# Layer 1's expert outputs: one written row per token and choice, weights loaded by row pairs, early sums fetched by pairs of tiles

## The chip, the cores and the metric

The kernel runs on one core of one Trainium2 chip. The metric is device time in microseconds. A core has five engines that matter here, each with its own instruction queue worked off in order: TensorE (PE, with its weight loads shown apart as PEld), VectorE (DVE), ScalarE (ACT), GpSimd (POOL) and SyncE (SP). SyncE computes nothing: it issues most of the DMAs. GpSimd issues the indirect DMAs, which gather or scatter rows by an index per partition.

## The reference, cut to what matters

Two layers, each of graph attention over a dense mask and then a mixture of experts, on 2708 nodes of 256 features, in fp32. Layer 0's mixture has 8 experts of hidden width 1024, layer 1's has 16 of width 512. A token goes to its two best experts. The part that the change concerns is this:

```python
# layer 1's mixture; x is the layer-normed node, K = 2
topk_vals, topk_idx = jax.lax.top_k(x @ gate_w + gate_b, K)
topk_w = jax.nn.softmax(topk_vals, axis=-1)          # the two weights of a token add up to 1
h = jax.nn.relu(jnp.einsum('bsh,ehf->bsef', x, w1) + b1)
expert_out = jnp.einsum('bsef,efh->bseh', h, w2) + b2
sel = jnp.take_along_axis(expert_out, topk_idx[:, :, :, None], axis=2)
y = x + jnp.sum(topk_w[..., None] * sel, axis=2)
out = (y - mean(y)) / jnp.sqrt(var(y) + EPS) * gamma + beta   # over the features
# and around it: nodes = nodes + out
```

## The kernel before, in words

The 2708 nodes are 22 tiles (T) of up to 128 partitions (P): 20 full ones and two of 74 rows (TAIL). W is 22 x 128 = 2816. Only the two chosen experts of a token are computed. The class `Router` ranks the choices, gives each (token, choice) a place in a list sorted by expert, and scatters a row there, into `rows_d` in DRAM (`scatter`, L681): 256 features and behind them the token's number (column D, from `tail`, L536), the expert and a weight. The list is cut into blocks of 128 rows of one expert each. Layer 0 works through 47 blocks for certain and layer 1 through 45 (`sure`); more would follow only if the data asked for them.

The class `Experts` does a block. `fetch` (L768) brings its 128 rows, `load_w1` (L755) and `load_w2` (L759) the expert's weights into one of three rooms (left out if the same expert is there already). `turn` transposes the rows on TensorE (L468) and ScalarE copies them. `hide` (L887) multiplies by w1, one chunk of 128 hidden columns at a time, its w1 chunk as the stationary operand; `bend` (L891) is the activation on ScalarE. `sum_hidden` (L902 for the bias, L905) multiplies by w2. `weigh` makes from the row's last columns `side` (L879: +0.5 or -0.5, by which of the token's choices this block's expert is) and on ScalarE the weight `w` (L881). `scaled` (L909, L911) makes `yo`, the weighted output, out of the PSUM. `add` (L916) is an indirect DMA on GpSimd which adds the 128 rows into `sums`, at the tokens' numbers. Even and odd blocks have a tensor each, so two chains exist, and within a chain an add waits for the one before it, since both can hold the same rows.

Layer 1's two sums are made by `sums_d` (L514 ff.): the second is filled with a row of nothing for all nodes and the first only for its filler rows (L518, two DMAs, the bigger 2,944 KB). The first gets its start from `store` (L932 to L935), which writes each tile's layer-normed rows, so that the sum of both tensors is x + moe. `points1` calls it (L1873), tile after tile, between attention and routing.

After the stream the rows come back: y_all has a place for each of the two tensors, y_all[:, 0] and y_all[:, 1]. GpSimd adds them (L1963 early, L1998 late), DVE takes mean and variance (L434, L435), a reciprocal root by a chain of small operations, and two operations per tile (L1973 and L1975 early, L2011 and L2013 late) that also add the node. Three parts follow each other: early group 1 (tiles 0 to 5), whose rows are complete after block 35; early group 2 (tiles 6 to 11), complete after block 38; and the late tiles 12 to 21, complete only at the end. Both early groups lie in `early_last` (from L1950), beside the last blocks, and the late ones in `last1` (from L1990). `early_out` (L1984) writes an early group's result.

The order of work on TensorE, ScalarE, DVE and SyncE in layer 1 is fixed when the program is built. `Clock` is a planner: each piece of work is a Python generator that yields an engine with an assumed duration, or a mark to wait for, and the planner places the instructions in the order of its own modelled times. So a figure such as

```python
                yield "DVE", 0.7
                yo = self.scaled(b, ps, weights.pop(b))
```

costs nothing itself but sets where in DVE's queue `scaled` stands. GpSimd's order is left to the scheduler. `experts1.rest()` follows the stream: on all five engines it loads the number of blocks in use (L948) and branches over the rest (L951). What is written behind it, the late loads among them, stands behind that branch in each queue. On SyncE the order at the end is: output writes of group 1, the branch, the ten late loads, the output writes of group 2.

Of the kernel before, what the change touches and what calls it, by code (L numbers as in the profile page):

```python
# [9 lines left out]
F32 = mybir.dt.float32  # L10
# [12 lines left out]
P = 128  # L23
# [123 lines left out]
def kernel(  # L147
# [374 lines left out]
    class Router:  # L522
# [4 lines left out]
        def __init__(self, layer, E, groups, w_gate, b_gate):  # L527
            self.w_gate, self.b_gate, self.E, self.layer = w_gate, b_gate, E, layer
            self.blocks = NB = blocks_of(E)
            self.rows_d = dram.tile([NB * P, RW], F32, name=f"rows_d{layer}")  # L530
            self.logits = sm.tile([P, T, E], F32, name=f"logits{layer}")
            nc.gpsimd.memset(self.logits, 0.0)
            self.hot = sm.tile([P, T, 2, E], BF16, name=f"hot{layer}")
            self.place = sm.tile([P, T, 2], I32, name=f"place{layer}")
            self.tail = sm.tile([P, T, 3], F32, name=f"tail{layer}")
            nc.gpsimd.iota(self.tail.bitcast(I32)[:, :, 0], pattern=[[P, T]], base=0,  # L536
                           channel_multiplier=1)

            self.room, self.page, self.next = (
                kept(f"{name}{layer}", 0.0, E) for name in ("room", "page", "next"))  # L540

            self.ends = sm.tile([P, len(groups), E], F32, name=f"ends{layer}")
            nc.gpsimd.memset(self.ends, 2.0 ** 22)
            self.groups, self.xt, self.ps, self.rows = groups, {}, {}, {}
            self.moves, self.reads, self.done = [], [], 0
# [174 lines left out]
    class Experts:  # L720
# [5 lines left out]
        def __init__(self, layer, router, w1, b1, w2, func, sums, tags, xg, xt, bias, sure):  # L726
# [6 lines left out]
            self.rooms, self.rows, self.known, self.planned, self.stages = {}, {}, 0, 0, []  # L733
            self.last_add, self.adds, self.early_reads = {}, ([], []), ([], [])
            self.b1_rows = w1x.rearrange("p c f -> p (c f)")[:E, :self.F]
            self.taken, self.sure = taken_of[layer], sure
# [18 lines left out]
        def load_w1(self, b):  # L755
            nc.sync.dma_start(self.rooms[b % 3][0], self.w1[bass.ds(self.e, 1)].rearrange(
                "o (c p) f -> p (o c) f", p=P), **self.when)

        def load_w2(self, b):  # L759
            nc.sync.dma_start(self.rooms[b % 3][1], self.w2[bass.ds(self.e, 1)].rearrange(  # L760
                "o (c p) d -> p (o c) d", p=P), **self.when)

# [21 lines left out]
        def plan(self, upto, bank=None):  # L784
# [72 lines left out]
            for f in range(self.FC):  # L857
                nc.tensor.matmul(ps[:, f], self.b1_rows[:, f * P:(f + 1) * P], hot[:E],
                                 start=True, stop=True)
# [9 lines left out]
        def turn(self, b):  # L869
            xt = self.xt_tile()  # L870
            ps = ps_tile("tr_ps", self.t_tag)[:, :D].rearrange("p (c n) -> p c n", n=P)
            nc.scalar.copy(xt, turn_rows(self.rows[b][:, :D], P, ps))
            return xt

        def weigh(self, b):

            xg = self.rows[b]
            side, w = (self.pool.tile([P, 1], F32, name=nm, bufs=3) for nm in ("side", "w"))
            nc.vector.tensor_scalar(side, xg[:, D + 1:D + 2], mine_of[:, b:b + 1], -0.5,  # L879
                                    op0=OP.is_equal, op1=OP.add)  # L880
            nc.scalar.activation(w, xg[:, D + 2:D + 3], AF.Tanh, scale=side)  # L881
            return w

        def hide(self, b, f, xt, ps):
            w1_b = self.rooms[b % 3][0]
            for c in range(DC):
                nc.tensor.matmul(ps[:, :P], w1_b[:, c, f * P:(f + 1) * P], xt[:, c, :],  # L887
                                 start=(c == 0), stop=(c == DC - 1))
# [19 lines left out]
        def scaled(self, b, ps, w):  # L908
            nc.vector.tensor_scalar(w, w, 0.5, 0.5, op0=OP.mult, op1=OP.add)  # L909
            yo = self.pool.tile([P, D], F32, name="yo", bufs=4)  # L910
            nc.vector.tensor_scalar(yo, ps[:, :D], w, None, op0=OP.mult)  # L911
            return yo

        def add(self, b, yo):
            k = b % 2
            ins = nc.gpsimd.indirect_dma_start(  # L916
# [41 lines left out]
        def stream(self, clock, stages, bank, acc, xrs, los, wides, widened, started):  # L958
# [47 lines left out]
            def turn(b):  # L1006
# [3 lines left out]
                yield "PE", 0.4  # L1010
                turn_rows(self.rows[b][:, :D], P, ps)
                clock.start(turned(b, ps, slot), 0)
# [17 lines left out]
            def weigh(b):  # L1030
                yield "DVE", 0.2
                yield "ACT", 0.3
                weights[b] = self.weigh(b)

            def finish(b, ps, slot):
                yield "DVE", 0.7
                yo = self.scaled(b, ps, weights.pop(b))
# [3 lines left out]
                clock.set(xr_slots.pop(b))  # L1041
                clock.set(self.added_at[b], 4.5)

# [656 lines left out]
    emb_sq, sig_sq, common = kept("emb_sq", 1.0), kept("sig_sq", 32.0), kept("common")  # L1700
    router1 = Router(1, E1, groups1, wg1, bg1)
    router1.fill()
    sums1 = [sums_d(f"sums1_{k}", zero=k == 1) for k in range(2)]
    experts1 = Experts(1, router1, L1_ffn_w1, L1_ffn_b1, L1_ffn_w2, AF.Relu, sums1,
# [100 lines left out]
    def points1(group):  # L1805
# [62 lines left out]
        for q, (t, r) in enumerate(group):  # L1868
# [3 lines left out]
            ln_f1.apply_s(router1.rows[t][:r, :D], x1[:r, t, :], t, r, shift[:, q:q + 1])  # L1872
            experts1.store(t, r, router1.rows[t][:r, :D])  # L1873
            if q % 2:
# [70 lines left out]


    EARLY_LAST = ((tiles[:6], 36), (tiles[6:12], 39))
    assert ENDS1[:2] == (6, 12) and list(early1.values()) == [8, 20] and E1 == 16

    def early_last(group, done):  # L1950

        yield experts1.added_at[done - 1]
        mark, lo, n = Mark(), group[0][0], len(group)
        if lo:
            yield experts1.loaded
            yield experts1.fetched
        for k in range(2):
            experts1.early_read(k, fetch_rows(y_all[:, k, lo:lo + n], sums1[k], group), done)
        clock.moved(mark, 0.8 * n, 2.5)
        yield mark  # L1960
        for t in range(lo, lo + n, 2):
            yield "POOL", 1.3
            nc.gpsimd.tensor_tensor(y_all[:, 0, t:t + 2], y_all[:, 0, t:t + 2],  # L1963
# [6 lines left out]
        for t, r in group:  # L1970
# [5 lines left out]
                                           op1=OP.add)  # L1976
        if not lo:
            yield experts1.loaded
            yield experts1.fetched
            early_out(group)  # L1980

    def early_out(group):
        for (t, _), _ in zip(group[::2], group[1::2]):
            nc.sync.dma_start(of_pair(out, t), y_all[:, 1, t:t + 2])  # L1984

    def load_y(group, k):
        lo = group[0][0]
        fetch_rows(y_all[:, k, lo:lo + len(group)], sums1[k], group)

# [47 lines left out]

    for group in late_last:
        load_y(group, SURE1 % 2)
    for group, mark in zip(late_last, loads):  # L2040
        load_y(group, 1 - SURE1 % 2)
        clock.moved(mark, 0.4 * len(group), 2.0)
    early_out(tiles[6:12])
    for group, mark in zip(late_last, loads):
# [33 lines left out]
```

## Time and profile before

| | |
|---|---|
| timed runs, median (lowest to highest) | 1162.97 us (1161.6 to 1166.65), 3 runs |
| profiled execution, its own time | 1136.56 us |
| its span; mean granted TensorE clock | 1134.8 us; 0.958 |
| PE, PEld busy | 1023.5 us (90%), 909.0 us (80%) |
| DVE, ACT, POOL busy | 541.9 us (48%), 572.7 us (50%), 367.1 us (32%) |
| DMA | 238.96 MB, 165,461 packets, mean 211 GB/s |
| L911, `yo`: 92 on DVE | 483 ns each |
| L916, accumulating add: 45 in layer 1, on POOL | 1569 ns each, landing after 4.6 us (median) |
| L887, weight loads, layer 0 (1504) and layer 1 (480) | 193 and 200 ns each |

The profile is of one execution; all its times are microseconds from the span's start. Its stages are, roughly: 0 to 120 the front, 120 to 330 attention of layer 0, 330 to 630 the experts of layer 0, 630 to 880 attention and routing of layer 1 (with routing going on beside the first blocks), 880 to 1094 the experts of layer 1, and 1094 to 1135 the end. The last matmul of the 45th block ends at 1093.84. A row of groups gives busy time and mean duration, and then the idle time that the engine had just before these instructions, with the instruction that ended most of it. A row of waits gives who waited, for what, the total, how many times, and the longest. Since engines overlap, a row's busy time is not its price: that is what it adds to the chain that ends last.

### The profile page before, as it was taken

How to read it: one execution, taken by the hardware profiler on the slowest of the kernel's cores; microseconds unless marked ns; L12 is line 12 of the kernel's file. 1: busy time of each engine (PE TensorE's matmuls, PEld its weight loads, DVE VectorE, ACT ScalarE, POOL GpSimd, SP SyncE). 2: the span in 40 equal slices, each digit the busy share in tenths (PEclk: the TensorE clock that was granted, in tenths of full speed). 3: DMA queues.
4: the chain of work that ended last, by engine and by line, in shares of the span. 5: the costliest groups of instructions: out<-in, count | busy, mean ns of one | idle time of the engine just before them, and what ended most of it. 6: DMA issues, size and time to landing. Idle time of an engine off the chain costs nothing. (4 is left out here: it accounts for less than half of the span.)

```text
span 1134.8 us, 21254 instructions
## 1 busy us (share of the span) xinstructions
PE 1023.5 (90%) x6665; PEld 909.0 (80%) x6665; DVE 541.9 (48%) x2083; ACT 572.7 (50%) x1599; POOL 367.1 (32%) x417
## 2 busy tenths in 40 slices
PE   5999999998999999999999999998984888999950
PEld 3788888886889999999998853898984787898840
DVE  7778888887420111111111235647777552122368
ACT  4867667664524444444443357536754543444320
POOL 7531112111242222212222350253345166433442
PEclk9999999999989999999999999999897889999985
DMA  9965354431889999999899959400225477787974
GB/s 289 288 242 177 136 175 156 166 95 58 303 251 295 327 326 322 323 306 321 257 311 335 340 160 278 150 1 6 76 84 153 124 215 188 187 213 178 282 194 133
DMA packets 165461, 238.96 MB, mean 211 GB/s; under 512 B 11035, under 2 KB 140374, under 8 KB 162632
## 3 DMA queue, kind: packets, MB, share of 16 engines
q1 hardware_dynamic: 146524, 214.09, 57.9%
q0 software_dynamic: 18816, 23.42, 10.6%
q8 instruction: 56, 0.92, 0.3%
q14 instruction: 65, 0.53, 0.2%
HBM read 205.54 MB, written 54.99 MB: 230 GB/s over the span
## 5 line engine op out<-in xcount | busy, mean ns | idle before, releaser
L911 DVE TENSOR_SCALAR yo<-out_ps,w 128x256 f32<-128x256 f32 x92 | 44.5, 483 | 402.4 <-PE out_ps L905 401.9
L1246 PE MATMUL att_ps<-g_all,z 128*128 128x257 f32 (+3 forms) x968 | 223.6, 383 | 0.0
L905 PE MATMUL out_ps<-room,ht 128*128 128x256 f32 x872 | 201.1, 383 | 0.0
L1246 PEld LDWEIGHTS att_ps<-g_all,z 128*128 128x128 f32 (+3 forms) x968 | 174.9, 186 | 29.6 <-issue 3.1
L887 PEld LDWEIGHTS hid_ps<-xt,room 128*128 128x128 f32 x1504 | 176.4, 193 | 7.3 <-issue 2.5
L887 PE MATMUL hid_ps<-xt,room 128*128 128x128 f32 x1504 | 177.7, 277 | 4.2 <-DMA room<-in_L_ffn_W_dram 3.7
L905 PEld LDWEIGHTS out_ps<-room,ht 128*128 128x128 f32 x872 | 162.7, 192 | 21.3
L1232 ACT ACTIVATE zr<-e_bc,minus_one,g_all 128x256 f32<-128x256 f32 (+3 forms) x242 | 130.4, 591 | 46.4 <-DVE z L1235 45.8
L916 POOL DMA_INDIRECT sums<-yo,xg x43 | 66.8, 1554 | 235.0 <-DVE side L879 173.4
L891 ACT ACTIVATE ht<-hid_ps,w_t 128x128 f32<-128x128 f32 x376 | 128.7, 364 | 28.0 <-PE hid_ps L887 8.8
L681 POOL DMA_INDIRECT rows_d<-xr,place x88 | 92.2, 1048 | 121.0 <-DVE xr L450 76.9
L1649 PE MATMUL att_ps<-half,wide_mask 128*128 128x258 f32 (+1 forms) x968 | 124.5, 290 | 2.5 <-ACT h_all L1586 1.5
L1649 PEld LDWEIGHTS att_ps<-half,wide_mask 128*128 128x128 f32 (+1 forms) x968 | 121.5, 195 | 3.9 <-ACT h_all L1586 2.4
L1235 DVE SCALAR_TENSOR_TENSOR z<-zr,mask_t 128x256 f32<-128x256 f32 (+3 forms) x242 | 96.9, 422 | 29.6 <-ACT zr L1232 18.3
L916 POOL DMA_INDIRECT sums<-yo,xr x45 | 70.6, 1569 | 118.0 <-DMA sums<-yo,xr 30.0
L891 ACT ACTIVATE ht<-hid_ps,w1x 128x128 f32<-128x128 f32 x180 | 62.4, 363 | 88.6 <-PE hid_ps L887 85.0
L881 ACT ACTIVATE w<-xg,side 128x1 f32<-128x1 f32 x43 | 12.7, 294 | 169.2 <-DVE side L879 169.2
L1525 POOL CAST wide_mask<-mask_t 128x1408 fp32r<-128x1408 fp8e4 x31 | 42.5, 1375 | 101.6 <-PE att_ps L1649 67.5
L887 PE MATMUL hid_ps<-lo,wide_mask 128*128 128x128 f32 x480 | 63.4, 287 | 5.6 <-DMA wide_mask<-in_L_ffn_w_dram 4.7
L887 PEld LDWEIGHTS hid_ps<-lo,wide_mask 128*128 128x128 f32 x480 | 60.6, 200 | 9.4 <-issue 6.5
L905 PE MATMUL out_ps<-wide_mask,ht 128*128 128x256 f32 x240 | 59.6, 393 | 0.0
L468 PE MATMUL tr_ps<-ident,xr 128*128 128x128 f32 (+1 forms) x214 | 38.2, 289 | 22.2 <-DMA xr<-rows_d 13.9
(292 smaller groups left out, 1325.0 us busy)
## 6 DMA issues: line engine op xcount, KB each, us to landing
room<-in_L_ffn_W_dram SPq DMA_DIRECT2D x94, 1024.0 KB
wide_mask<-in_L_ffn_w_dram SPq DMA_DIRECT2D x60, 512.0 KB
room<-in_adj_dram SPq DMA_DIRECT2D x20, 1354.0 KB
room<-in_L_ffn_w_dram SPq DMA_DIRECT2D x30, 512.0 KB
rows_d<-nobody SPq DMA_DIRECT2D x1, 7511.0 KB
rows_d<-nobody SPq DMA_DIRECT2D x5, 1295.0 KB
sums<-nobody SPq DMA_DIRECT2D x2, 2944.0 KB
xr<-rows_d SPq DMA_DIRECT2D x45, 129.5 KB
```

The costliest lines, as they stand in the source:

```text
L468: nc.tensor.transpose(ps[:, c, :r], src[:, c * P:(c + 1) * P], ident[:r, :r])
L681: ins = nc.gpsimd.indirect_dma_start(out=self.rows_d[:, :], in_=self.rows[t][:r], in_offset=None, out_offset=bass.IndirectOffsetOnAxis(ap= ...
L887: nc.tensor.matmul(ps[:, :P], w1_b[:, c, f * P:(f + 1) * P], xt[:, c, :], start=(c == 0), stop=(c == DC - 1))
L891: nc.scalar.activation(ht[:, f, :], ps[:, :P], self.func, bias=self.bias[:, f, b:b + 1])
L905: nc.tensor.matmul(ps[:, :D], ht[:, f, :], self.rooms[b % 3][1][:, f, :], start=False, stop=(f == self.FC - 1))
L911: nc.vector.tensor_scalar(yo, ps[:, :D], w, None, op0=OP.mult)
L916: ins = nc.gpsimd.indirect_dma_start(out=self.sums[k][:, :], in_=yo, in_offset=None, out_offset=bass.IndirectOffsetOnAxis(ap=self.rows.pop ...
L1232: nc.scalar.activation(zr[:k, :n], e_bc[:k, lo:lo + n], AF.Relu, bias=minus_one[:k], scale=g_all[:k, j, D + 1:D + 2])
L1235: nc.vector.scalar_tensor_tensor(z[:k, :n], zr[:k, :n], 1.0, mask_t[:k, j // 2, lo:lo + n, j % 2], op0=OP.add, op1=OP.mult)
L1246: nc.tensor.matmul(accs[i][:r, :D + 1], z[:k, q * P:q * P + r], g_all[:k, j, :D + 1], start=(j == 0), stop=(j == LAST))
L1525: nc.gpsimd.tensor_copy(m, src)
L1649: nc.tensor.matmul(accs[i][:, :D + 2], wide_masks[i, j % 2][:k, j // 2, :], half_k[:k, j, :], start=(j == 0 and half_k is halves[0]), stop ...
```

## The change

There are four parts.

1. In layer 1 a single DRAM tensor `sums1` of 2W rows takes the place of the two sums. The row of choice k of the node at partition p of tile t is k W + p T + t, so that one partition's tiles lie side by side. `weigh` computes this index (`spot`, on DVE) from `side` and from the row's `tail` column, which now holds p T + t + W/2. `put` is a plain indirect scatter, without adding and without a wait on earlier blocks; filler rows get an index beyond the bound and aren't written. `scaled` gets one more DVE operation, which adds w times the block's input row, because the two weights of a token add up to 1; so the filling of the sums and `store` go.
2. In both layers a partition's share of w1 becomes two neighbouring rows, and of w2 two neighbouring rows per chunk pair, in one run. Transposes, hide and the bias then read every second column of their stationary operand (`turn_row`, `part`).
3. The early sums are fetched two tiles at a time, each pair after a mark one block later than the pair before, both choices in one DMA (`load_y`). Group 2 no longer waits for the end of the loads and fetches before its own loads; both groups wait for it before `early_out`. The late loads are five DMAs in place of ten (the pair of 74 rows is split in two), and the call that wrote group 2's results after them goes: group 2 writes them inside the stream.
4. The planner's assumed durations follow: `weigh` 0.4, `finish` 1.1 on DVE, landing 3.0, and 1.6 for the move of a pair.

```diff
@@ -533,8 +533,12 @@
             self.hot = sm.tile([P, T, 2, E], BF16, name=f"hot{layer}")
             self.place = sm.tile([P, T, 2], I32, name=f"place{layer}")
             self.tail = sm.tile([P, T, 3], F32, name=f"tail{layer}")
-            nc.gpsimd.iota(self.tail.bitcast(I32)[:, :, 0], pattern=[[P, T]], base=0,
-                           channel_multiplier=1)
+            if layer:
+                nc.gpsimd.iota(self.tail[:, :, 0], pattern=[[1, T]], base=W // 2,
+                               channel_multiplier=T, allow_small_or_imprecise_dtypes=True)
+            else:
+                nc.gpsimd.iota(self.tail.bitcast(I32)[:, :, 0], pattern=[[P, T]], base=0,
+                               channel_multiplier=1)
 
             self.room, self.page, self.next = (
                 kept(f"{name}{layer}", 0.0, E) for name in ("room", "page", "next"))
@@ -732,6 +736,7 @@
             self.FC, self.NB = self.F // P, router.blocks
             self.rooms, self.rows, self.known, self.planned, self.stages = {}, {}, 0, 0, []
             self.last_add, self.adds, self.early_reads = {}, ([], []), ([], [])
+            self.spots = {}
             self.b1_rows = w1x.rearrange("p c f -> p (c f)")[:E, :self.F]
             self.taken, self.sure = taken_of[layer], sure
 
@@ -754,11 +759,12 @@
 
         def load_w1(self, b):
             nc.sync.dma_start(self.rooms[b % 3][0], self.w1[bass.ds(self.e, 1)].rearrange(
-                "o (c p) f -> p (o c) f", p=P), **self.when)
+                "o (p c) f -> p (o c) f", p=P), **self.when)
 
         def load_w2(self, b):
-            nc.sync.dma_start(self.rooms[b % 3][1], self.w2[bass.ds(self.e, 1)].rearrange(
-                "o (c p) d -> p (o c) d", p=P), **self.when)
+            room = self.rooms[b % 3][1].rearrange("p (q s) d -> p q (s d)", s=2)
+            nc.sync.dma_start(room, self.w2[bass.ds(self.e, 1)].rearrange(
+                "o (q p s) d -> p (o q) (s d)", p=P, s=2), **self.when)
 
         def load(self, b):
             self.choose(b)
@@ -855,7 +861,7 @@
             ps = ps[:, :self.FC * n].rearrange("p (f b) -> p f b", b=n)
             yield "PE", 0.2 * self.FC
             for f in range(self.FC):
-                nc.tensor.matmul(ps[:, f], self.b1_rows[:, f * P:(f + 1) * P], hot[:E],
+                nc.tensor.matmul(ps[:, f], self.part(self.b1_rows, f), hot[:E],
                                  start=True, stop=True)
             yield "ACT", 0.4
             if not lo:
@@ -869,22 +875,37 @@
         def turn(self, b):
             xt = self.xt_tile()
             ps = ps_tile("tr_ps", self.t_tag)[:, :D].rearrange("p (c n) -> p c n", n=P)
-            nc.scalar.copy(xt, turn_rows(self.rows[b][:, :D], P, ps))
+            nc.scalar.copy(xt, self.turn_row(b, ps))
             return xt
+
+        def turn_row(self, b, ps):
+            by_turns = self.rows[b][:, :D].rearrange("p (n c) -> p c n", c=DC)
+            for c in range(DC):
+                nc.tensor.transpose(ps[:, c], by_turns[:, c], ident)
+            return ps
+
+        def part(self, w, f):
+
+            return w.rearrange("p (q n s) -> p q s n", n=P, s=2)[:, f // 2, f % 2]
 
         def weigh(self, b):
 
             xg = self.rows[b]
             side, w = (self.pool.tile([P, 1], F32, name=nm, bufs=3) for nm in ("side", "w"))
+            if self.layer:
+                self.spots[b] = self.pool.tile([P, 1], I32, name="spot", bufs=5)
             nc.vector.tensor_scalar(side, xg[:, D + 1:D + 2], mine_of[:, b:b + 1], -0.5,
                                     op0=OP.is_equal, op1=OP.add)
             nc.scalar.activation(w, xg[:, D + 2:D + 3], AF.Tanh, scale=side)
+            if self.layer:
+                nc.vector.scalar_tensor_tensor(self.spots[b], side, -float(W), xg[:, D:D + 1],
+                                               op0=OP.mult, op1=OP.add)
             return w
 
         def hide(self, b, f, xt, ps):
             w1_b = self.rooms[b % 3][0]
             for c in range(DC):
-                nc.tensor.matmul(ps[:, :P], w1_b[:, c, f * P:(f + 1) * P], xt[:, c, :],
+                nc.tensor.matmul(ps[:, :P], self.part(w1_b[:, c], f), xt[:, c, :],
                                  start=(c == 0), stop=(c == DC - 1))
 
         def bend(self, b, f, ht, ps):
@@ -909,9 +930,24 @@
             nc.vector.tensor_scalar(w, w, 0.5, 0.5, op0=OP.mult, op1=OP.add)
             yo = self.pool.tile([P, D], F32, name="yo", bufs=4)
             nc.vector.tensor_scalar(yo, ps[:, :D], w, None, op0=OP.mult)
+            if self.layer:
+                nc.vector.scalar_tensor_tensor(yo, self.rows.pop(b)[:, :D], w, yo, op0=OP.mult,
+                                               op1=OP.add)
             return yo
 
+        def put(self, b, yo):
+
+            ins = nc.gpsimd.indirect_dma_start(
+                out=self.sums[0][:, :], in_=yo, in_offset=None,
+                out_offset=bass.IndirectOffsetOnAxis(ap=self.spots.pop(b), axis=0),
+                bounds_check=2 * W - 1, oob_is_err=False)
+            for other in [put for _, put in self.adds[0]] + self.early_reads[0]:
+                tc.declare_no_dep(ins.ins, other, reason="every choice of a token has its row")
+            self.adds[0].append((b, ins.ins))
+
         def add(self, b, yo):
+            if self.layer:
+                return self.put(b, yo)
             k = b % 2
             ins = nc.gpsimd.indirect_dma_start(
                 out=self.sums[k][:, :], in_=yo, in_offset=None,
@@ -1008,7 +1044,7 @@
                 slot = yield from bank.get()
                 ps = ps_tile("tr_ps", self.t_tag)[:, :D].rearrange("p (c n) -> p c n", n=P)
                 yield "PE", 0.4
-                turn_rows(self.rows[b][:, :D], P, ps)
+                self.turn_row(b, ps)
                 clock.start(turned(b, ps, slot), 0)
 
             def turned(b, ps, slot):
@@ -1028,18 +1064,18 @@
                     clock.set(ht_at[b])
 
             def weigh(b):
-                yield "DVE", 0.2
+                yield "DVE", 0.4
                 yield "ACT", 0.3
                 weights[b] = self.weigh(b)
 
             def finish(b, ps, slot):
-                yield "DVE", 0.7
+                yield "DVE", 1.1
                 yo = self.scaled(b, ps, weights.pop(b))
                 clock.set(slot)
                 yield "POOL", 1.6
                 self.add(b, yo)
                 clock.set(xr_slots.pop(b))
-                clock.set(self.added_at[b], 4.5)
+                clock.set(self.added_at[b], 3.0)
 
             def outputs(b):
                 slot = yield from acc.get()
@@ -1699,8 +1735,10 @@
     emb = h_all[:, :, :D]
     emb_sq, sig_sq, common = kept("emb_sq", 1.0), kept("sig_sq", 32.0), kept("common")
     router1 = Router(1, E1, groups1, wg1, bg1)
+    nc.gpsimd.iota(nobody[:, D:D + 1], pattern=[[0, 1]], base=W + W // 2, channel_multiplier=1,
+                   allow_small_or_imprecise_dtypes=True)
     router1.fill()
-    sums1 = [sums_d(f"sums1_{k}", zero=k == 1) for k in range(2)]
+    sums1 = [dram.tile([2 * W, D], F32, name="sums1")]
     experts1 = Experts(1, router1, L1_ffn_w1, L1_ffn_b1, L1_ffn_w2, AF.Relu, sums1,
                        ("wide", "wide", "acc"), lambda b: xr_tile(),
                        lambda: side.tile([P, D], F32, name="lo", bufs=2).rearrange(
@@ -1870,7 +1908,6 @@
             router1.rows[t] = xr_tile()
             yield "ACT", 0.6
             ln_f1.apply_s(router1.rows[t][:r, :D], x1[:r, t, :], t, r, shift[:, q:q + 1])
-            experts1.store(t, r, router1.rows[t][:r, :D])
             if q % 2:
                 clock.start(logits1(group[q - 1:q + 1], taken_at[lo][q // 2]), urgency(group))
         for mark in taken_at[lo]:
@@ -1944,21 +1981,26 @@
 
 
 
+    def load_y(group):
+
+        lo, hi = group[0][0], group[-1][0] + 1
+        src = sums1[0].rearrange("(k p t) d -> p k t d", k=2, p=P)
+        for a, b in parts_of_rows(group[0][1]):
+            ins = nc.sync.dma_start(y_all[a:b, :, lo:hi], src[a:b, :, lo:hi])
+        return ins
+
     EARLY_LAST = ((tiles[:6], 36), (tiles[6:12], 39))
     assert ENDS1[:2] == (6, 12) and list(early1.values()) == [8, 20] and E1 == 16
 
     def early_last(group, done):
 
-        yield experts1.added_at[done - 1]
-        mark, lo, n = Mark(), group[0][0], len(group)
-        if lo:
-            yield experts1.loaded
-            yield experts1.fetched
-        for k in range(2):
-            experts1.early_read(k, fetch_rows(y_all[:, k, lo:lo + n], sums1[k], group), done)
-        clock.moved(mark, 0.8 * n, 2.5)
-        yield mark
+        lo, n = group[0][0], len(group)
         for t in range(lo, lo + n, 2):
+            mark = Mark()
+            yield experts1.added_at[done - 1 + (t - lo) // 2]
+            experts1.early_read(0, load_y(tiles[t:t + 2]), done)
+            clock.moved(mark, 1.6, 2.5)
+            yield mark
             yield "POOL", 1.3
             nc.gpsimd.tensor_tensor(y_all[:, 0, t:t + 2], y_all[:, 0, t:t + 2],
                                     y_all[:, 1, t:t + 2], OP.add)
@@ -1974,18 +2016,13 @@
                                            op0=OP.subtract, op1=OP.mult)
             nc.vector.scalar_tensor_tensor(y, y, ln_y.rstd[:, t:t + 1], x1[:, t, :], op0=OP.mult,
                                            op1=OP.add)
-        if not lo:
-            yield experts1.loaded
-            yield experts1.fetched
-            early_out(group)
+        yield experts1.loaded
+        yield experts1.fetched
+        early_out(group)
 
     def early_out(group):
         for (t, _), _ in zip(group[::2], group[1::2]):
             nc.sync.dma_start(of_pair(out, t), y_all[:, 1, t:t + 2])
-
-    def load_y(group, k):
-        lo = group[0][0]
-        fetch_rows(y_all[:, k, lo:lo + len(group)], sums1[k], group)
 
     def last1(group, y_at):
 
@@ -2035,12 +2072,9 @@
     late_last = [tiles[12:14], tiles[14:16], tiles[16:20], tiles[20:22]]
     loads = [Mark() for _ in late_last]
 
-    for group in late_last:
-        load_y(group, SURE1 % 2)
     for group, mark in zip(late_last, loads):
-        load_y(group, 1 - SURE1 % 2)
-        clock.moved(mark, 0.4 * len(group), 2.0)
-    early_out(tiles[6:12])
+        load_y(group)
+        clock.moved(mark, 0.8 * len(group), 2.0)
     for group, mark in zip(late_last, loads):
         clock.start(last1(group, mark))
     clock.run()
```

## The prediction

> **What bounds the kernel now.** I read the page's span, then busy times cut by stage, then TensorE's waits in each stage, SyncE's waits, and last the timeline of the final 40 us. Busy times by stage (columns: us, then PE, PEld, DVE, ACT, POOL busy, granted clock, DMA share, GB/s):
>
> ```profile
> 330.00:600.00 270.00, 268.42 (x1830) 251.57 (x1830) 27.71 (x113) 113.16 (x360) 55.19 (x37) 0.99 0.96 304
> 900.00:960.00 60.00, 50.43 (x362) 44.80 (x361) 29.51 (x156) 23.09 (x75) 35.91 (x34) 0.94 0.69 179
> 960.00:1090.00 130.00, 124.52 (x851) 114.23 (x851) 39.53 (x148) 56.90 (x189) 53.73 (x35) 0.99 0.82 221
> 1090.00:1135.00 45.00, 3.84 (x20) 2.97 (x17) 30.96 (x95) 3.96 (x12) 14.58 (x11) 0.58 0.50 137
> ```
>
> Both expert streams (rows 1 and 3) belong to TensorE: 268 of 270 us and 125 of 130. DVE is at 40 of 130 us in the second, so DVE work there lies under matmuls. The last 45 us have almost no matmul: DVE, 31 us, carries them. So only two things move the end: what holds TensorE in layer 1's stream, and the order of DVE, SyncE and GpSimd after about 1083 us. TensorE's waits, 880 to 1095 us (total, times, longest):
>
> ```profile
> PE tr_ps L468 <- DMA xr<-rows_d: 13.9, 2, 12.3
> PE hid_ps L887 <- DMA wide_mask<-in_L_ffn_w_dram: 4.7, 4, 3.2
> PE hid_ps L887 <- DMA room<-in_L_ffn_w_dram: 3.5, 5, 1.4
> PE number_ps L826 <- DVE fresh_bf L822: 3.1, 1, 3.1
> ```
>
> The 12.3 us waits for the first rows after the router's scatters and stays. The rest is some 13 us. In layer 0 TensorE waited for weights only 3.7 us in all. SyncE's queue, 780 to 960 us:
>
> ```profile
> SPq L935 <- ACT xr L459: 34.2, 7, 14.9
> ```
>
> Line 935 is `store`: 24 writes of rows into the sums. The last six issue at 920.92 to 928 us, and the next fetch of rows follows at 929.32, ahead of TensorE's second tr_ps wait (1.59 us, at 931.6). The end, SyncE and then DVE:
>
> ```profile
> 1085.56 4.76 SPq L1984 DMA_DIRECT2D out_dram<-mask_t  x3
> 1102.91 1.41 SPq L1428 DMA_DIRECT2D mask_t<-sums  x3
> ...
> 1109.41 4.79 SPq L1984 DMA_DIRECT2D out_dram<-mask_t  x3
> ```
> ```profile
> 1100.37 0.43 DVE L434 BATCH_NORM_STATS2 bn<-mask_t 128x6 f32<-128x256 f32 x1 [6.00 <-POOL mask_t L1963]
> ...
> 1112.42 1.42 DVE L1975 SCALAR_TENSOR_TENSOR mask_t<-mask_t,rstd_y,h_all 128x256 f32<-128x256 f32 x1
> 1113.98 0.43 DVE L434 BATCH_NORM_STATS2 bn<-mask_t 128x6 f32<-128x256 f32 x1
> ```
>
> The ten late loads (1102.91 to 1108.9) go ahead of the three output writes of early group 2 (1109.41), so the late sums are there when DVE finishes group 2, and DVE goes on at 1113.98 with no idle time. That order is what the change turns round.
>
> [...]
>
> **The change, part by part.** The sum is against the profiled 1136.56 us (span 1134.8); the timed median, 1162.97, stands 2.3% above, and I add the difference to it.
>
> *Weights by row pairs (both layers).* Counts don't change. Packets of w1 and w2 halve in number. [...] TensorE is busy 268.42 of 270, so it can return at most the 3.7 us waited: -1 taken (0 to -3.7). [...] Hide's time is about 47 x 3.73 + 45 x 1.95 = 263 us, so each 1% on it is +2.6 us; a read at half speed would be over 100 us. I take 0.
>
> *Puts instead of accumulating adds (layer 1).* L916 takes 1569 ns on GpSimd and lands in 4.6 us; the plain scatter (L681) takes 1048 ns and lands in 3.5 to 3.9. So 45 x 0.5 = 23 us less on POOL, and no 30.0 us of waits. All hidden: POOL is at 54 of 130 us. In the stream: 0.
>
> *DVE pays for it.* Per block, spot (128x1, as side: 0.20 us) and x*w+yo (128x256, as L1936: 0.48), 45 x 0.68 = 31 us. Between 960 and 1090 this makes 40 into 60 of 130 us: cover remains, and yo frees the PSUM before the new line. Between 895 and 910, where the plan of the layer is made and TensorE already waits 3.1 us for DVE's fresh_bf, two blocks' extra may lie in the way: +1.5 (0 to +3).
>
> *Fills and stores.* Two fills (21.4 us of SyncE's issue at 683, with nothing due until 781) and 24 stores go. Hidden, except the SyncE lag of 920 to 929: -1.6 at 931.6 and, if SyncE then keeps its lead, the 3.25 us wait at 956.3 with the slow first hide after it (3.11 against 1.95): -1.6 to -6; I take -3. An added iota on POOL lies in an idle stretch: 0.
>
> *Early loads by pairs.* Six DMAs of 512 KB, spread through w1/w2 of blocks 40 to 44, instead of four of 768 KB. The 1.4 us TensorE wait at 1075.8 stands beside the old ones: -0.7 (0 to -1.4). TensorE's end (1093.8) thus moves by -1 + 1.5 - 3 - 0.7 = about -3, from -10 to +3.
>
> *DVE's order at the end.* Before, group 1 starts its statistics in the gap of block 40 (1075). In the built program they stand after the new line of block 41, about 1083.8, and side and spot of block 43 wait behind them. From there, at the rows' durations (pair statistics 1.22, newton chain 2.3 to 2.4, 0.92 a tile): group 1's statistics to 1088.8 with their waits, newton to 1091.2, blocks 42 to 44 between tiles 0 and 1 to 1096.4, tiles 2 to 5 to 1100.2, group 2's statistics to about 1104.8 with POOL beside them, newton and 12 operations to 1112.6. Before: 1113.9. The 6.00 us wait on POOL vanishes, and group 1's later start eats it: -1.3.
>
> *SyncE's order at the end: the step that decides.* The output writes of both groups now come before the block count's load, the branch over the rest, and the late loads. Queued behind group 2's last write, which waits for DVE (1112.6), are: its issue 0.4; load and branch 0.9 (1090.4 to 1091.3 before); [...], 5.0 us on SyncE before, 1.1 on DVE, 2.9 on POOL, taken as 2.5 (0.5 to 5); issue to landing 2.3; POOL's add of a pair, 1.26. So DVE starts the late part at 1112.6 + 7.4 = 1120.0 instead of 1113.98: +6.0 (+3.5 to +9.5). Five loads instead of ten save only issue time that was hidden. The late part (17.65 us of DVE, then 3.2 to the end) is the same.
>
> Sum: -3 + 6 = **+3 us**, span about 1138; 1162.97 + 3 = **1166 us**. Nearly everything else that the change removes was hidden.
>
> **Rivals.** (a) *Slower by a strided stationary read.* No trace row excludes it[...]. From 2% on hide it decides alone (+5 us); 5% gives +13, 1180 us. It would show as LDWEIGHTS of L887 longer than 193 ns and a layer-0 block above 7.36 us. (b) *Faster through the removed queueing.* If the stores had held SyncE back for the whole ramp, the waits of 1.6, 4.7, 3.5 and the slow hides go (-10), and [...] (+3.5): -7, 1156 us. For: the 929.32 fetch. Against: 4.7 and 3.5 us come in nine pieces, and TensorE is back at 0.96 by 960. (c) *Slower through DVE in the plan chain[...]:* +3 there instead of +1.5, SyncE's saving not realised (0), tail +9.5: +12, 1175 us. [...] (d) *Packets matter in the timed runs.* They are 26 us over the profiled one, unexplained[...].
>
> **How the numbers follow.** A difference under 0.5% (5.8 us) is about what a measurement here can't tell from none. My forecast +3 has 0.50; within it some 0.30 stay inside 0.5%, 0.18 fall above, since the tail's +6 reaches the end whole where upstream savings fail, 0.02 below. (a) 0.12, slower. (b) 0.13, faster. (c) 0.17, 0.15 of it slower. (d) 0.08, 0.07 of it faster. Together faster 0.22, same 0.33, slower 0.45. The range 1152 to 1183 takes in the tail's and the ramp's ends and a 5% stride; left out are a half-speed read (0.08), more than 11 us gained (0.07), and odd waits. The likeliest case alone spans 1161 to 1173.
>
> **What would show it.** Right: a DVE gap of 5 to 8 us between group 2's last operation and the late statistics, ended by POOL's late add, with SyncE's late loads issued after 1113; L916 near 1.0 us; no POOL wait for sums in the stream; LDWEIGHTS of L887 still near 193 ns; layer-0 period 7.36 us; the late part 17 to 18 us. The prediction is wrong if hide's pitch moves (a), if TensorE ends layer 1 more than 7 us earlier (b), or if the 900 to 960 us stretch loses TensorE time to fresh_bf (c).

## The result and the profile after

The changed kernel takes 1192.03 us (median of 4 runs, 1189.6 to 1196.42) against 1164.4 us before (4 runs, 1161.6 to 1166.65): a ratio of 1.0245, with a 95% interval of 1.0214 to 1.0276. It is slower by about 28 us, where the forecast said 3 us slower and a range up to 1183 us. Timed once more beside the kernel before, it came to 1.0201 (1.0168 to 1.0234), some 23 us. The loss is of 2.0 to 2.5%.

The two first profiles can't be subtracted from each other. Kernels were compared on one chip at a time, and the median of the kernel before was 1135.8, 1157.5, 1164.3 and 1136.2 us in the four later comparisons, the first and last of which were on the same chip. The first profile of before (1136.56 us) is like those of the quicker chip, the first of the changed kernel (1189.6 us) like those of the slower ones. So where spans and ends are compared below, and nothing else is said, the traces are the second profiles of both, taken on one chip: 1138.94 and 1157.68 us.

First the changed kernel's busy times by stage, from its first profile (columns as before: us, PE, PEld, DVE, ACT, POOL busy, clock, DMA share, GB/s):

```profile
330.00:600.00 270.00, 267.26 (x1780) 250.86 (x1779) 27.33 (x113) 111.89 (x348) 53.78 (x36) 0.99 0.91 293
960.00:1090.00 130.00, 120.90 (x824) 111.37 (x823) 51.88 (x205) 54.91 (x178) 37.72 (x41) 0.99 0.56 179
1090.00:1135.00 45.00, 39.80 (x264) 36.48 (x262) 24.22 (x79) 17.35 (x57) 14.84 (x15) 0.99 0.76 256
1135.00:1188.00 53.00, 0.00 (x0) 0.00 (x0) 37.40 (x105) 3.28 (x9) 10.91 (x9) 0.50 0.29 104
```

Layer 0's row tells nothing of the cost: TensorE is as busy as before, because it is busy for longer per block. The DMA share is 0.91 in place of 0.96 (0.93 in the second profile), with fewer bytes moved per us (293 in place of 304 GB/s), and it returned nothing. The two middle rows lie in layer 1's expert stream, where DVE, at 52 of 130 us, stays under the matmuls. The last row is the end without matmuls, some 53 us long, of which DVE works 37. The timeline of TensorE in layer 0 shows the first cause, in the first profile of before and then of after; the second profiles have the same durations:

```profile
427.86 3.73 PE L887 MATMUL hid_ps<-xt,room 128*128 128x128 f32 x32
431.43 0.38 PE L468 MATMUL tr_ps<-ident,xg 128*128 128x128 f32 x2
431.65 0.27 PE L902 MATMUL out_ps<-b,hot_of 96*128 96x256 bf16 x1
431.77 3.62 PE L905 MATMUL out_ps<-room,ht 128*128 128x256 f32 x16
```
```profile
430.41 3.92 PE L908 MATMUL hid_ps<-xt,room 128*128 128x128 f32 x32
434.17 0.39 PE L884 MATMUL tr_ps<-ident,xg 128*128 128x128 f32 x2
434.40 0.27 PE L923 MATMUL out_ps<-b,hot_of 96*128 96x256 bf16 x1
434.51 3.62 PE L926 MATMUL out_ps<-room,ht 128*128 128x256 f32 x16
```

Hide's 32 matmuls, which now read w1 at a step of two, take 3.92 us and not 3.73. The matmuls with w2, whose stationary operand is not strided, stay at 3.62. The block period goes from 7.36 to 7.56.

The second cause is at the end. SyncE and then DVE, in the second profile after:

```profile
1121.45 2.17 SPq L2025 DMA_DIRECT2D out_dram<-mask_t  x2
1127.68 2.84 SPq L1989 DMA_DIRECT2D mask_t<-sums  x5
```
```profile
1122.77 0.48 DVE L2017 SCALAR_TENSOR_TENSOR mask_t<-mask_t,rstd_y,h_all 128x256 f32<-128x256 f32 x1
1132.74 0.43 DVE L434 BATCH_NORM_STATS2 bn<-mask_t 128x6 f32<-128x256 f32 x1 [9.49 <-POOL mask_t L2035]
```

The five late loads are issued at 1127.68, about 4 us after group 2's last output write, and DVE, finished with group 2 at 1123.25, stands still for 9.49 us (9.6 to 9.7 in the three other traces of kernels with this order at the end). Before, the loads went first and there was no such gap.

Measured from TensorE's last matmul, the traces line up as follows (us; statistics are the first L434 of each part):

| | layer 0, first hide to last output | TensorE's end | group 1 | group 2 | late part | end of span |
|---|---|---|---|---|---|---|
| before, second profile | 362.1 | 1096.2 | -19.7 | +6.9 | +21.4 | +40.9 |
| changed, second profile | 370.2 | 1101.3 | -8.5 | +10.8 | +31.5 | +54.7 |

So 5.1 us of the difference of 18.9 between these spans lie ahead of TensorE's end, and 13.8 behind it. Single traces scatter: in the first profile of before, layer 0's stretch took 366.6 us, and in the three other traces with the changed order the end is 56.4 to 56.7 us long.

### The profile page after: what moved, and what is told of

Same layout as the page of the kernel before. It is cut to its first block, busy times and chain, and to the rows that moved or that the text cites. A ratio compares the mean times of both kernels' runs of the same rounds, so it can differ in the third digit from the quotient of the medians.

```text
span 1187.9 us, 21355 instructions
## 1 busy us (share of the span) xinstructions
PE 1042.8 (88%) x6665; PEld 928.8 (78%) x6665; DVE 575.0 (48%) x2173; ACT 576.4 (49%) x1599; POOL 341.5 (29%) x418
## 5 line engine op out<-in xcount | busy, mean ns | idle before, releaser
L908 PEld LDWEIGHTS hid_ps<-xt,room 128*128 128x128 f32 x1504 | 185.0, 197 | 10.5 <-issue 4.6
L908 PE MATMUL hid_ps<-xt,room 128*128 128x128 f32 x1504 | 186.7, 282 | 7.1 <-DMA room<-in_L_ffn_W_dram 2.2
L912 ACT ACTIVATE ht<-hid_ps,w_t 128x128 f32<-128x128 f32 x376 | 131.1, 364 | 37.5 <-PE hid_ps L908 10.4
L912 ACT ACTIVATE ht<-hid_ps,w1x 128x128 f32<-128x128 f32 x180 | 65.3, 367 | 95.2 <-PE hid_ps L908 70.2
L940 POOL DMA_INDIRECT sums<-yo,spot x45 | 44.2, 982 | 151.6 <-DVE yo L934 77.5
L908 PE MATMUL hid_ps<-lo,wide_mask 128*128 128x128 f32 x480 | 66.5, 294 | 5.4 <-DMA wide_mask<-in_L_ffn_w_dram 3.3
L908 PEld LDWEIGHTS hid_ps<-lo,wide_mask 128*128 128x128 f32 x480 | 63.8, 205 | 9.3 <-issue 5.3
L926 PEld LDWEIGHTS out_ps<-wide_mask,ht 128*128 128x128 f32 x240 | 46.5, 204 | 6.4
```

Of the source, the lines that this page charges most:

```text
L908: nc.tensor.matmul(ps[:, :P], self.part(w1_b[:, c], f), xt[:, c, :], start=(c == 0), stop=(c == DC - 1))
L912: nc.scalar.activation(ht[:, f, :], ps[:, :P], self.func, bias=self.bias[:, f, b:b + 1])
L926: nc.tensor.matmul(ps[:, :D], ht[:, f, :], self.rooms[b % 3][1][:, f, :], start=False, stop=(f == self.FC - 1))
L940: ins = nc.gpsimd.indirect_dma_start(out=self.sums[0][:, :], in_=yo, in_offset=None, out_offset=bass.IndirectOffsetOnAxis(ap=self.spots.po ...
```

## The experiments

**Both kernels again.**

> The kernel before, unchanged, profiled once more. Its first profile (1136.6 us) lies 26 us below its timed median, so a sum against that profile may compare a lucky execution with an ordinary one. Theory 1 (the first profile was an unusually undisturbed one): the new profile lies near 1163 us and shows waits or stalls of TensorE of some 26 us in all that the first lacks. Rival (profiled executions of this kernel are always shorter than timed ones): again near 1137 us.

It took 1138.94 us, near the first profile, beside a timed median of 1135.8: neither account holds as written. The timed executions moved with the chip, and a profile on this chip is no shorter than they are.

> The changed kernel, profiled once more. Its first profile has a 10.5 us stop of TensorE, ScalarE and DVE at 882 us that no work in the trace accounts for. Theory 1 (the stop is chance, and not of the change): this profile is without it, or has it elsewhere, and the time varies by about 10 us with it. Rival (the change causes it): the stop is there again at the same place, 10 us long, and not in the kernel before.

It took 1157.68 us, without the stop: TensorE's wait for hot_f was 2.0 us, as in before. Later profiles on the slower chips had the stop in every kernel, and none on the quicker chip had it. Here it is in TensorE's waits of the kernel before with w1's pairs alone:

```profile
PE bias_ps L858 <- DVE hot_f L850: 11.4, 1, 11.4
```

The stop goes with the chip (three are on record), not with the change.

**Row pairs, alone and left out.** The pairs alone, put into the kernel before:

```diff
-                "o (c p) f -> p (o c) f", p=P), **self.when)
+                "o (p c) f -> p (o c) f", p=P), **self.when)
...
-                nc.tensor.matmul(ps[:, :P], w1_b[:, c, f * P:(f + 1) * P], xt[:, c, :],
+                nc.tensor.matmul(ps[:, :P], self.part(w1_b[:, c], f), xt[:, c, :],
```

(with w2's load, the transposes and the bias as in the change)

> The kernel before with the weight row pairs alone (w1, w2, transposes, hide and bias read at a step of two). Theory 1 (the strided stationary read costs 0.19 us per 32 matmuls, as the first trace after shows): +13 us, a layer-0 hide of 3.92 us in place of 3.73, a layer-1 hide of 2.04 in place of 1.95. Rival (the longer hide is the chip's, not the stride's): 0 to -4 us, hide as before.

1.0114 (1.0075 to 1.0153): 1149.17 against 1135.84 us, +13.3. Hide took 3.92 us in layer 0 and 2.04 in layer 1, over 47 and 45 blocks 13 us more. The theory holds.

> The changed kernel with the weights loaded and read as before, all else as changed. Theory 1 (row pairs cost 13 us, and the rest of the 28 us comes from layer 1's order at the end and from DVE): about +14 us against the kernel before, hide back at 3.73 and 1.95 us. Rival (the row pairs are all of it): 0 to +4 us. Rival (the stride costs nothing): +28 us as the changed kernel.

1.0158 (1.0119 to 1.0197): 1152.87 against 1135.84, +17.0. So the pairs are not all of it. In this trace TensorE ends at 1092.6, no later than in before (1093.8 and 1096.2), and the end of the span is 56.7 us behind it against 41: without the pairs, the whole loss lies in the end. The pairs alone and everything else alone add up to 30 us, beside 28 and 23 measured for the whole change: near the one and above the other. Whether the two overlap is not settled.

**Which half of the pairs.** w1 by pairs alone makes the loads' packets larger and the transposes strided, but hide reads contiguously:

> The kernel before with w1 by row pairs alone: the load and the transposes change, hide reads contiguously. Theory (the 13 us belong to hide's stationary operand, which w2's pairs make strided): 0 to +1.5 us (transposes 0.39 us in place of 0.38 for each of 92 blocks), hide back at 3.73 and 1.95. Rival (the larger packets or the transposes cost it): +5 or more.

1.0003 (0.9984 to 1.0022), and hide at 3.73 us. Neither w1's larger packets (156,373 in all in place of 165,461) nor the transposes (0.40 us in place of 0.38) count, within 0.2%; the strided read of hide, which w2's pairs bring about, does. (w2's own packets can't be made larger without it; hide's 13 us account for the whole loss of the pairs.)

**A wider step.** w2 by four rows a partition, so hide reads at a step of four fp32:

```diff
+            room = self.rooms[b % 3][1].rearrange("p (q s) d -> p q (s d)", s=4)
...
+            return w.rearrange("p (q n s) -> p q s n", n=P, s=4)[:, f // 4, f % 4]
```

> The kernel before with w2 by four neighbouring rows, so that hide and the bias read their stationary operand at a step of four fp32 (16 bytes) instead of two; w1 and the transposes are as before. Theory 1 [...]: hide grows well beyond 3.92 us, +25 us or more. Rival 1 (the cost is one of any stride): +13 as with pairs. Rival 2 ([...] the pairs' 13 us come from elsewhere): hide jumps only here.

1.2094 (1.2022 to 1.2166), +241 us. The weight loads of hide in layer 0, from the groups of the trace with pairs and then of this one (busy us, mean ns):

```profile
L898 PEld LDWEIGHTS hid_ps<-xt,room 128*128 128x128 f32 x1504 | 184.0, 197 | 5.6 <-ACT w L892 1.8
L898 PEld LDWEIGHTS hid_ps<-xt,room 128*128 128x128 f32 x1504 | 354.5, 329 | 1.9 <-ACT xt L873 0.8
```

329 ns against 197 at a step of two and 193 contiguous, and 7.52 us for the 32 matmuls. Steps of 1, 2 and 4 give 3.73, 3.92 and 7.52 us. Theory 1, with +25 us or more, is nearest: a step of two already costs 5%, and a step of four (16 bytes) doubles the time. What in the read makes this the runs don't show.

**The order at the end.** One thing put back in the changed kernel:

```diff
-        yield experts1.loaded
-        yield experts1.fetched
-        early_out(group)
+        if not lo:
+            yield experts1.loaded
+            yield experts1.fetched
+            early_out(group)
...
+    early_out(tiles[6:12])
```

> The changed kernel with one thing put back: early group 2's three output writes stand behind the late loads again, outside the stream. Theory (the late loads, queued behind those writes and the branch, leave DVE idle for 9.5 us): the gap goes, and the late part loses the 2.4 us it spends beside GpSimd's late adds; -10 to -12 us against the changed kernel, +10 to +13 against the one before. Rival (DVE's added work, not SyncE's order, sets the end, and the gap only moves): -0 to -3, so about +20 against the one before.

1.0111 (1.0051 to 1.0172): 1171.07 against 1157.46 us, +13 and not the 23 or more of the changed kernel (which was compared on other chips). DVE's waits from group 2 on have no late gap any more, only what the branch costs:

```profile
DVE bn L434 <- DVEq L987: 0.7, 1, 0.7
DVE bn L434 <- issue: 0.2, 1, 0.2
```

The late part starts 26.5 us behind TensorE's end instead of 31.5 to 33.6, and the span ends 47.4 us behind it instead of 54.7 to 56.7. The late part itself is back at 20.8 us. The theory holds in size, but 47.4 is not yet 41.

The same order, alone, in the kernel before:

```diff
-        if not lo:
-            yield experts1.loaded
-            yield experts1.fetched
-            early_out(group)
+        yield experts1.loaded
+        yield experts1.fetched
+        early_out(group)
...
-    early_out(tiles[6:12])
```

> The kernel before with that order alone: group 2's output writes inside the stream, ahead of the branch and of the late loads. Theory: a gap of 7 to 10 us opens in DVE between group 2 and the late part, +8 to +12 us in all. Rival (it needs the pair loads or the puts as well): 0 to +2.

1.0130 (1.0069 to 1.0190): 1171.92 against 1157.46, +14.5, more than the +8 to +12 expected. DVE's waits:

```profile
DVE bn L434 <- POOL mask_t L1997: 15.2, 1, 15.2
DVE bn L434 <- POOL mask_t L1963: 5.9, 1, 5.9
```

The gap is 15.2 us, longer than in the changed kernel, whose loads are five and not ten: from the first load's issue to GpSimd's first late add 8.1 us pass here and 3.8 there. The order needs neither puts nor pair loads to do its harm.

**What is left.** The changed kernel timed again, and then without pairs and with the order put back:

> The changed kernel, timed on the same chip as the two that follow. Theory (13 us from the row pairs' stride, 15 from the end, less some 5 gained before): +22 us against the kernel before, as in its second profile. Rival (the 28 us of the first comparison are the right size, and the 10.5 us stop of its profile belongs to the change): +28, with the stop in the trace.

1.0201 (1.0168 to 1.0234), +23 us: the size fits the theory, though the stop was in this trace too (12.6 us).

> The changed kernel with both found causes taken out: weights loaded and read as before, and group 2's output writes behind the late loads. Theory (nothing else of the change costs): -3 to +2 us against the kernel before. Rival (the puts' added DVE work and group 1's later start cost too): +4 to +7, with group 1's statistics starting some 9 us before TensorE's end and the end 46 us or more behind it.

1.0033 (1.0014 to 1.0052), +3.9 us. That lies between the two accounts, and the trace speaks for the rival: group 1's statistics start 8.7 us before TensorE's end (18.7 and 19.7 in before) and the span ends 47.3 us behind it. So a third cost remains, in DVE's order, which the part on the prediction takes up.

**Early loads issued together,** in the kernel just above:

```diff
-        for t in range(lo, lo + n, 2):
-            mark = Mark()
-            yield experts1.added_at[done - 1 + (t - lo) // 2]
+        yield experts1.added_at[done - 1]
+        marks = [Mark() for _ in range(lo, lo + n, 2)]
+        for t, mark in zip(range(lo, lo + n, 2), marks):
             experts1.early_read(0, load_y(tiles[t:t + 2]), done)
             clock.moved(mark, 1.6, 2.5)
+        for t, mark in zip(range(lo, lo + n, 2), marks):
             yield mark
```

> As the one before it, and an early group's three pair loads are issued together once the block that completes the group has landed, instead of one after the other. In the built order group 1's first statistics then stand one to two blocks earlier in DVE's queue, and two of group 2's pairs beside the last blocks. Theory (the serial pair loads delay DVE's early work, which then sets the end): 3 to 6 us less than the one before it, so -4 to 0 against the kernel before. Rival (DVE waits elsewhere then): as the one before it.

1.0014 (0.9999 to 1.0028): some 2 us less than the kernel above, by these two medians. The trace says more than the time does. Group 1's statistics start 28.5 us ahead of TensorE's end and the span ends only 35.2 us behind it, but TensorE's end itself came later. SyncE's timeline:

```profile
1099.94 0.37 SPq L761 DMA_DIRECT2D wide_mask<-in_L_ffn_w_dram  x1
1104.09 1.40 SPq L1988 DMA_DIRECT2D mask_t<-sums  x3
1106.27 0.02 SPq L765 DMA_DIRECT2D wide_mask<-in_L_ffn_w_dram  x1
1107.13 0.35 SPq L777 DMA_DIRECT2D xr<-rows_d  x1
```

TensorE's, and DVE's with one line of ScalarE's:

```profile
1108.00 0.38 PE L468 MATMUL tr_ps<-ident,xr 128*128 128x128 f32 x2
1117.68 3.76 PE L907 MATMUL hid_ps<-lo,wide_mask 128*128 128x128 f32 x16 [7.46 <-ACT lo L1053]
```
```profile
1111.74 3.23 DVE L2015 SCALAR_TENSOR_TENSOR mask_t<-mask_t,mv_y,gamma 128x256 f32<-128x256 f32 x1
1116.32 0.21 DVE L896 TENSOR_SCALAR side<-xr,mine_of 128x1 f32<-128x1 f32 x1
1116.56 0.29 ACT L898 ACTIVATE w<-xr,side 128x1 f32<-128x1 f32 x1 [8.89 <-DVE side L896]
```

Group 2's loads wait for a put until 1104.09, with block 43's w2 and block 44's rows queued behind them. It looks like the cause of the 7.46 us for which TensorE stands, but it isn't: the rows of the block that TensorE waits for were transposed at 1108.00. What it waits for is ScalarE's copy of them (`lo`), which stands in ScalarE's queue behind `w`, and `w` waited 8.89 us for DVE's `side`. DVE, without a pause, first worked on group 1's tiles, one operation of which took 3.23 us instead of 0.48.

**Those loads moved back.** Group 2's loads two blocks later, and in the second kernel group 1's one block later as well:

```diff
-        yield experts1.added_at[done - 1]
+        yield experts1.added_at[done - 1 + (2 if lo else 0)]
```

(`2 if lo else 1` in the second)

> As the kernel with joint early loads, but group 2's loads are issued two blocks later (the built order puts them behind the last weight load). Theory (in that kernel SyncE waited 3.8 us for a put ahead of a weight load and a fetch, and TensorE then stood 7.5 us before block 44): TensorE's 7.5 us stop goes, the tail stays near 36 to 38 us, so -4 to -7 us against the kernel before. Rival (group 2's later statistics push the end back by as much): 0 to +2.

0.9991 (0.9975 to 1.0006): 1136.15 against 1136.18 us. TensorE's 7.46 us stop is gone, and the span ends 39.1 us behind TensorE. That doesn't make the theory's reason right: moving the loads also moved the planner's order on DVE, and the trace above has the cause there. The kernel equals the kernel before and doesn't beat it: part of the shorter tail was given back, since group 2's loads now start when the last weights are issued and its statistics 5.0 us after TensorE's end, not 8.4 us before it.

> As the kernel with joint early loads, but group 1's loads one block later and group 2's two blocks later. Theory as for the other: no SyncE wait for puts ahead of weights, -3 to -6 us against the kernel before, a tail 1 to 3 us longer than with group 1 at its earlier place. Rival: 0 to +2.

1.0036 (1.0018 to 1.0053). Here TensorE waits for weights at the place where group 1's loads now stand:

```profile
1079.51 3.76 PE L907 MATMUL hid_ps<-lo,wide_mask 128*128 128x128 f32 x16 [4.18 <-DMA wide_mask<-in_L_ffn_w_dram]
```

Both expectations were too hopeful. No kernel tried is faster than the one before.

## Why the prediction was wrong

The direction was right and the size was not: +3 us forecast, +28 and +23 measured. The forecast's own points, in its order:

*Weights by row pairs.* That the strided read costs nothing was an estimate of the author's with no measured number behind it, and it is the step that failed most. Alone it is +13.3 us of measured time. A step of two costs 5% of hide here and a step of four 102% (3.73, 3.92, 7.52 us); why, no run shows. The working had the right number at hand: "5% gives +13, 1180 us" stood under rival (a), with a chance of 0.12. A free read had been taken for likely although no row of the profile had such a read, and each percent was priced at 2.6 us. The forecast's own sign of being wrong, a moved pitch of hide, is what came. That the larger packets would return next to nothing, because TensorE paces layer 0 (268 of 270 us busy), was right: 1.0003 for w1's pairs.

*Puts instead of adds.* L916's successor (L940) takes 982 ns, near the 1048 taken from L681. The trace of the kernel without pairs shows TensorE's end 1 to 4 us earlier than before, about the gain forecast for the ramp; but two profiles of before differ by 2.3 us at that point, so this gain is not shown.

*DVE's order at the end.* -1.3 was forecast for the time that DVE is done with group 2; it is done 22.0 us after TensorE's end in the second profile after and 23.9 to 24.0 in the three other traces with this order, against 21.3 and 20.0 in the two profiles of before, and 18.8 in the forecast. The forecast missed what DVE loses beside GpSimd. In the second profile after, one of the small new operations takes 2.73 us while GpSimd adds two pairs (1102.70 to 1105.18, 2.48 us):

```profile
1102.23 0.21 DVE L897 TENSOR_SCALAR side<-xr,mine_of 128x1 f32<-128x1 f32 x1
1102.48 2.73 DVE L901 SCALAR_TENSOR_TENSOR spot<-side,xr 128x1 int32<-128x1 f32 x1
```

Elsewhere this operation takes 0.16 us. In the three other traces, and in both kernels with the writes put back, two of them are that long; so in the first profile after:

```profile
1123.74 3.12 DVE L901 SCALAR_TENSOR_TENSOR spot<-side,xr 128x1 int32<-128x1 f32 x1
1134.58 2.72 DVE L901 SCALAR_TENSOR_TENSOR spot<-side,xr 128x1 int32<-128x1 f32 x1
```

That is 5.5 us more than the two take elsewhere, in a stretch in which DVE has hardly a pause. The kernel with both causes taken out has the same two (3.11 and 2.72 us), and its late part starts 26.2 us after TensorE's end in place of 20.1 to 21.4. So most of what is left there fits these two; no run takes them out alone. The before trace had shown the effect on L1973 (1.50 us in place of 0.48, beside a GpSimd add of 1.26 us at 1110.85), and the forecast had allowed for it in the statistics alone.

*SyncE's order at the end.* The mechanism was the right one and its terms were too small: a DVE gap of 7.4 us, so +6.0 net, was forecast, and 9.49 measured, with +13.8 for the whole end. Of the terms, the issue, the branch and the time allowed for SyncE behind it (0.4, 0.9 and 2.5, together 3.8) measured about 4.4 from DVE's end to the loads (1123.25 to 1127.68). What the queue waits for behind the branch, 5.0 us on SyncE in before, no run shows; the 2.5 was an estimate within the measured 1.1 to 5.0. Issue to landing was put at 2.3 us and is 3.8 (1127.68 to GpSimd's add at 1131.45). The late part itself, taken as unchanged, takes 23.3 us and not 19.5 to 20.8, since GpSimd's late adds now run beside it (three of DVE's operations take 1.2, 1.2 and 1.6 us in place of 0.16 and 0.48 beside the three adds from 1137.50 on, 3.70 us). Put in numbers of the table: start of the late part +10.1, its length +3.7, together the 13.8. The 10.1 alone is past the +9.5 that the forecast gave as this step's upper end.

*The rest.* The plan chain (+1.5 forecast) can't be told from noise: TensorE's wait for fresh_bf was 3.1 and 4.5 us in the two profiles of before and 3.7 in the second after. Rival (c), a longer tail, was half right; (b) and (d) were wrong. The range ended at 1183 because a 5% stride and a long tail had been held as separate cases; both came true, the tail longer than thought, and their sum was outside it.

## What to carry to other kernels

A read pattern that no row of the profile shows has no measured price, so don't take it for free: price it per percent, and if a few per cent of a 263 us row would decide the result, measure that row alone first. At the end of a kernel, list what stands in each issuing queue behind an instruction that waits for a computing engine; results that are written early gain nothing if the loads of the next part queue behind them. Before a wait is named the cause of a stop, follow the stop back through each queue: a small operation that another engine needs may stand behind bulk work. Two dangers that share a cause or can both come true belong in one case of the forecast too, with their sum in the range.

## What the runs showed of the hardware

- A stationary fp32 operand of TensorE read at a step of 1, 2 and 4 elements (the kernel before, then with both weights by pairs, then with w2 by fours): layer 0's 32 hide matmuls of 128 columns in 3.73, 3.92 and 7.52 us; a weight load of 193, 197 and 329 ns.
- The 128x1 DVE operation that makes `spot`, 0.16 us elsewhere, takes 2.7 to 3.1 us beside two GpSimd adds of 128x512 (2.5 us the two).
- The same program differs by 2.5% between the three chips on record: medians of the kernel before of 1136 us twice on one, and of 1157 and 1164 us on two others. In the slower comparisons each of the seven traces, and the first of the changed kernel too, has a stop in which TensorE waits 11.4 to 12.6 us for hot_f in place of 2.0, at the same place of the program. In the first trace of the changed kernel and in that of w1's pairs alone, ScalarE waits there 11.7 and 11.4 us for what the view calls "remote"; the first trace of before has no such wait. Its cause was not found; that it stands in kernels of both kinds speaks against the change.
